# A Mamba block on one core: three tiles normalized inside the next tile's product, the first chunk's taps in one slot, later projections spread 1, 2, 1

## The chip, the cores and the metric

The kernel runs on one core of a Trainium2 chip. Times are device microseconds of one execution; the kernel before took 3516.83 us (median of three, 3515.82 to 3521.38). The engines are PE (TensorE, matrix products), PEld (its weight loads), DVE (VectorE), ACT (ScalarE), POOL (GpSimd) and SP, which only issues DMAs here. Each engine works through its instructions in a fixed order.

## The reference, cut to what matters

Four graph layers run one after the other on 3327 nodes with 256 features, each with a residual sum and a layer norm. The change lies in layer 1, a graph convolution followed by a Mamba block:

```python
h = jax.nn.relu(adj @ x @ gcn_w + gcn_b)
h = (h - mu) * lax.rsqrt(var + EPS) * ln_g + ln_b      # per node
xz = h @ w_in
xc, z = (xz[:, :D_INNER], xz[:, D_INNER:])             # D_INNER = 512
xconv = sum((xpad[k:k + L] * conv_w[:, k] for k in range(D_CONV))) + conv_b   # D_CONV = 4
u = jax.nn.silu(xconv)
dbc = u @ w_xp
dt = jax.nn.softplus(dbc[:, :DT_RANK] @ w_dt + b_dt)
# for each of 16 states, along the nodes: hst = exp(dt * A) * hst + dt * B * u;  y += hst * C
y = (ys + u * D_skip) * jax.nn.silu(z)
return y @ w_out
```

The nodes are a sequence for the Mamba block, so the scan over them cannot be cut without a carry.

## The kernel before, in words

**Tiles and chunks.** The 3327 nodes are 26 tiles of 128. `convolve` (L318) makes the graph convolution one tile at a time: 26 products of 128x128 by 128x256 over the adjacency (52 passes on PE), a copy to SBUF on ACT, two transposes, the product with `gcn_w`, the bias, relu with its sum, and the sum of squares. Three steps end a tile: `measure` (three small POOL instructions for the scale and the offset of the norm), `norm` (one ACT instruction) and `turn` (two PE transposes into the PSUM bank "ps", two ACT evacuations into the chunk's `hT`). `convolve` is a generator: it gives control back after each three products and reports units of work, 122 to a tile.

The scan takes the tiles in seven chunks of 3, 4, 4, 4, 4, 4 and 3 tiles. A chunk has 16 slots, one for each state. A slot does four scans on DVE (one per group of 128 channels, `scan`), each fed by a decay that ACT writes (`decay`, exp of dt times A, into one of two PSUM buffers), then one DVE product over all groups (`product`, buffer hc, two of them), which PE then adds up with transposing products into the y banks (`add_up`). POOL makes dt times u times B for the slot after the next (`feed`).

**The head of the next chunk.** While a chunk is scanned, `Head` prepares the next: `project` (four groups; PE product, ACT copy into `xc`, ACT first tap into `u`), `taps` (three DVE instructions for each group), `silu`, `mixed` (the product with `w_xp`, and two DMAs that write B and C out), `step_size`, `exponentials`, `rounding`, `logarithms`, `finish`. Chunk 0's own head runs before the scan begins. In which slot each step stands is the table `plan(c)` (L246): for chunk 0, one projection in each of slots 1 to 4, taps in slots 7, 8 and 9, silu 9, mixed 10; for later chunks, projections 0 and 1 in slot 5, 2 and 3 in slot 6, taps in slots 7 and 8. Before the projections of chunk c's slots the tiles of chunk c+1 must be there (`pump`). `gate_input` makes the z half of a tile. Projections, gate inputs, `mixed` and step sizes of the chunks from 2 on all go through the one bank "ps"; head 1 uses "y3" and "ps" in turn (`bank`, L298).

**What sets the order.** Before the scan loop the framework's list scheduler orders what is written. In the loop (`pinned`) DVE and POOL instructions keep the written order, and on ACT the decays, norms, silus and exponentials form one chain in written order (`in_turn`, L279). PE and the rest of ACT are ordered by the scheduler, mostly as written. How much of the convolution stream is written in each slot is the planner's: `duty` (L403) estimates the PE units of a slot (12 for a plain slot of chunk 0, 32 more with `mixed` there), `quota` (L422) fills the slots between two due times up to a common level, 96 units ahead. In the stream, the three end steps of a tile stand behind the next tile's third, seventh and eighth group of three products (the list `rest`, L374), but only in the loop. For tiles 0 to 6, which are written before it, they follow the tile at once (L375).

Of the kernel before, what the change touches and what calls it, by code (L numbers as in the profile page):

```python
# [18 lines left out]
P = 128  # L19
# [4 lines left out]
JC = 9  # L24
# [6 lines left out]
NG = DI // P  # L31
# [16 lines left out]
def gnn_kernel(ctx: ExitStack, tc: tile.TileContext, n: int, a: dict, out: bass.AP):  # L48
    nc = tc.nc
    nt = -(-n // P)  # L50
# [59 lines left out]
    def aggregate(atp, psum, it, rhs, cols, jh=JH, source=None):  # L110

        acc = psum.tile([P, cols], F32, name="acc")
        for j0 in range(0, nt, jh):
            m = min(jh, nt - j0)
            if source is not None:
                nc.sync.dma_start(rhs[:, j0:j0 + m, :D], source[:, j0:j0 + m, :])
            at = atp.tile([P, jh, P], F32, name="at")
            nc.sync.dma_start(at[:, :m, :], a["adjT"][it][:, j0:j0 + m, :])
            for j in range(m):
                nc.tensor.matmul(acc, at[:, j, :], rhs[:, j0 + j, :],  # L120
                                 start=(j0 + j == 0), stop=(j0 + j == nt - 1))
        return acc
# [35 lines left out]
    with tc.tile_pool(name="l1b", bufs=1) as wpool, tc.tile_pool(name="l1at", bufs=2) as l1at:  # L158
        X0 = F[:, :, :D]


        with tc.tile_pool(name="l0", bufs=1) as pool, tc.tile_pool(name="l0w", bufs=2) as work, \
# [4 lines left out]
            for it in range(nt):  # L167
                if it:
                    acc = aggregate(atp, psum, it, xa, D + 1)
                else:  # L170
                    acc = aggregate(atp, psum, it, xa, D + 1, J0, a["x"])
# [10 lines left out]
                for k in range(4):  # L182
                    nc.tensor.matmul(po, xt[:, k, :] if k < 2 else mt[:, k - 2, :], w0[:, k, :],
                                     start=(k == 0), stop=(k == 3))
# [7 lines left out]
        with tc.tile_pool(name="l1aw", bufs=1) as cwork, tc.tile_pool(name="l1c", bufs=2) as ch, \  # L192
# [53 lines left out]
            def plan(c):  # L246


                if c == 0:
                    return dict(project={g + 1: (g,) for g in range(NG)}, taps={7: (0,), 8: (1,), 9: (2, 3)}, gates={5: (0, 1), 6: (2,)},  # L250
                                silu=9, mixed=10, sizes={10: (0, 1), 11: (2, 3)}, exps=(11, 12), log=13)
                return dict(project={5: (0, 1), 6: (2, 3)}, taps={7: (0, 1), 8: (2, 3)}, gates={7: (0, 1), 8: (2, 3)},
                            silu=8, mixed=9, sizes={9: (0,), 10: (1, 2), 11: (3,)}, exps=(11, 12), log=13)

            ends = []
# [6 lines left out]
            pinned = False  # L262
# [13 lines left out]
            ten, act = nc.tensor, nc.scalar  # L276
# [29 lines left out]
            def spread(y, sm, nm, sq):  # L306

                act.activation(nm, sm, AF.Copy, scale=-1.0 / D)
                junk = cwork.tile([P, D], F32, name="m")
                act.activation(junk, y, AF.Square, bias=nm, accum_out=sq)  # L310

            def scales(rs, nb, nm, sq):

                gps.tensor_scalar(rs, sq, 1.0 / D, EPS, op0=ALU.mult, op1=ALU.add)
                gps.tensor_tensor(rs, rs, mhalf[:, :rs.shape[1]], op=ALU.pow)
                gps.tensor_tensor(nb, nm, rs, op=ALU.mult)

            def convolve():  # L318

                rest = []  # L320
                full = 0
                for it in range(nt):
                    if it < ends[1] // P and it % 2 == 0 and it:
                        cb = ypsum.tile([P, DI], F32, name="y3")
                    else:
                        cb = cpsum.tile([P, DI], F32, name="cb")
                    acc, tp = cb[:, :D], cb[:, D:]
                    for j in range(nt):
                        if j % JC == 0:
                            m = min(JC, nt - j)  # L330
                            at = l1at.tile([P, JC, P], F32, name="at")
                            nc.sync.dma_start(at[:, :m, :], a["adjT"][it][:, j:j + m, :])
                        ten.matmul(acc, at[:, j % JC, :], X0[:, j, :], start=(j == 0), stop=(j == nt - 1))  # L333
                        if j % JM == JM - 1 and j < nt - 1:
                            if rest:
                                step = rest.pop(0)
                                step()
                                full += step is turn
                            yield full, 4 * JM
                    m = cwork.tile([P, D], F32, name="m")  # L340
                    act.copy(m, acc)
                    yield full, 8
                    for k in range(2):
                        ten.transpose(tp[:, k * P:(k + 1) * P], m[:, k * P:(k + 1) * P], ident)
                    mt = cwork.tile([P, D], F32, name="m")
                    act.copy(mt, tp)
                    yield full, 4
                    for k in range(2):
                        ten.matmul(acc, mt[:, k * P:(k + 1) * P], gw[:, k, :], start=(k == 0), stop=False)
                    ten.matmul(acc, one, gb, start=False, stop=True)  # L350
                    h = cwork.tile([P, D], F32, name="hn")
                    rs, nb, nm, sm, sq = (small.tile([P, 1], F32, name=x) for x in ("rs", "nb", "nm", "sm", "sq"))
                    act.activation(h, acc, AF.Relu, accum_out=sm)  # L353
                    spread(h, sm, nm, sq)

                    def measure(rs=rs, nb=nb, nm=nm, sq=sq):
                        scales(rs, nb, nm, sq)

                    def norm(h=h, rs=rs, nb=nb):
                        turn_or_not = in_turn if pinned else lambda op, *x, **k: op(*x, **k)  # L360
                        turn_or_not(act.activation, h, h, AF.Identity, scale=rs, bias=nb)

                    def turn(it=it, h=h):
                        c = next(x for x in range(nch) if it * P < ends[x])
                        i = it * P - starts[c]
                        if i == 0:
                            hTs[c] = ch.tile([P, D // P, WC], F32, name="hT", bufs=3)
                        pt = psum.tile([P, WC], F32, name="ps")
                        for k in range(2):
                            ten.transpose(pt[:, k * P:(k + 1) * P], h[:, k * P:(k + 1) * P], ident)  # L370
                        for k in range(2):
                            act.activation(hTs[c][:, k, i:i + P], pt[:, k * P:(k + 1) * P], AF.Identity,
                                                 scale=g1[:, k:k + 1], bias=b1[:, k:k + 1])
                    rest = [*2 * [lambda: None], measure, *3 * [lambda: None], norm, turn]  # L374
                    if not pinned:  # L375
                        for step in (measure, norm, turn):
                            step()
                        rest = []
                        full += 1
                    yield full, 14  # L380
                for step in rest:
                    step()
                    full += step is turn
                    yield full, 12

            stream = convolve()
            done = taken = 0
            ready, valued, valuing = 0, 0, iter(())
# [14 lines left out]
            def duty(c, s):  # L403


                m, n, b = tiles_of(c), tiles_of(c + 1), tiles_of(c - 1)
                p = plan(c)
                return 4 * m * (2 if s == 0 else 1) + 24 * (1 <= s <= b) + 16 * len(gates(c, s)) \
                    + 4 * n * len(p["project"].get(s, ())) + 8 * n * (s == p["mixed"]) + 2 * n * len(p["sizes"].get(s, ()))
# [4 lines left out]
            def gates(c, s):  # L414
                return [i for i in plan(c)["gates"].get(s, ()) if i < tiles_of(c)]

            def due(c):
                return c * DS + min(plan(c)["project"]) if c else 8
# [263 lines left out]
            pinned = True  # L682
# [104 lines left out]
            pinned = False  # L787
# [6 lines left out]
            for i in range(m):  # L794
                it = starts[nch - 1] // P + i
# [819 lines left out]
```

## Time and profile before

| | |
|---|---|
| median of three | 3516.83 us |
| profiled execution | 3519.38 us, its span 3517.5 us |
| layer 0 (span's start to 380) | PE 371.6 of 380 us |
| first tiles of layer 1 (380 to 441.9) | PE 55.6, ACT 31.8 of 61.9 us |
| Mamba scan and its tail, to 1340 | DVE 821.0, PE 754.1, ACT 612.7, POOL 532.2 of 898.1 us |
| the rest (layers 2 and 3) | PE 2054.3, DVE 1470.3 of 2177.5 us |
| granted TensorE clock | 0.970 over the span |

The scan of chunk 0 begins at 441.9 us, chunk 1 at 588.4, chunk 2 at 728.5, chunk 3 at 868.6, chunk 4 at 1008.7, chunk 5 at 1146.5 and chunk 6 at 1277.7.

In the lines shown below, a line of the order of time gives the start and length in us, the engine, the source line, the operation, "out<-in", the shape and how many were merged; in brackets stands how long the engine stood idle before it and what ended that. Most DVE and POOL instructions of the loop, and the in-turn ones of ACT, carry a helper's line, L274 or L281, so that tile names tell them apart: h is a scan's output, hc the product's, u the taps', dA the decay. A line of who waited for whom gives the total us, the number of times and the longest.

### The profile page before, as it was taken

The numbers are of one execution on the slowest core, as the hardware profiler recorded it, in microseconds if no ns is written. First come the engines' busy times: TensorE is split into PE (matmuls) and PEld (weight loads), VectorE is DVE, ScalarE is ACT, GpSimd is POOL, SyncE is SP. The second block draws the span as 40 slices with busy tenths as digits, with TensorE's granted clock in tenths as the row PEclk, the third lists the DMA queues.
The fourth block names the chain that finished last, engine by engine and source line by source line (L and its number), as shares of the span: only waits on it lengthen the run. The fifth ranks groups of instructions, "written<-read, shape, count | busy, mean of one in ns | idle before, by whom it ended". The sixth has DMA issues, their size and how long they took to land. (4 is left out here: it accounts for less than half of the span.)

```text
span 3517.5 us, 43266 instructions
## 1 busy us (share of the span) xinstructions
PE 3235.5 (92%) x15597; PEld 2540.3 (72%) x15597; DVE 2370.4 (67%) x5245; ACT 1740.6 (49%) x2751; POOL 932.8 (27%) x942
## 2 busy tenths in 40 slices
PE   9999988988888766999899999999997999999996
PEld 7888766676676555888677878787775777777775
DVE  1111177999999997777454544444434999999996
ACT  0000356767667675111133333333336888888883
POOL 0000054666665653121100000000001243333332
PEclk9999998999999888999899999999999999999998
DMA  7443334334443222344321212121212112222220
GB/s 248 139 140 110 102 109 112 101 119 106 106 119 91 66 58 92 126 140 145 95 66 56 65 49 65 48 67 47 67 47 74 55 56 67 68 70 61 70 65 16
DMA packets 147577, 307.99 MB, mean 88 GB/s; under 512 B 19570, under 2 KB 68850, under 8 KB 147218
## 3 DMA queue, kind: packets, MB, share of 16 engines
q1 hardware_dynamic: 147346, 305.06, 29.7%
q8 instruction: 126, 2.06, 0.2%
q14 instruction: 105, 0.86, 0.1%
HBM read 294.36 MB, written 10.65 MB: 87 GB/s over the span
## 5 line engine op out<-in xcount | busy, mean ns | idle before, releaser
L274 POOL TENSOR_TENSOR h<-du,row 128x2048 f32<-128x2048 f32 (+1 forms) x110 | 465.7, 4233 | 339.3 <-DVE hc L274 270.8
L274 DVE TENSOR_TENSOR_SCAN h<-dA,carry,h 128x512 f32<-128x512 f32 (+1 forms) x384 | 448.7, 1220 | 19.8 <-ACT dA L281 19.7
L281 ACT ACTIVATE dA<-t,A_log 128x512 f32<-128x512 f32 (+1 forms) x448 | 292.3, 658 | 146.4 <-DVE h L274 143.4
L1058 PE MATMUL acc<-F,at 128*128 128x256 f32 x1352 | 353.5, 387 | 1.0 <-ACT q L832 0.6
L1091 PE MATMUL acc<-X,wt 128*128 128x256 f32 x1352 | 343.5, 390 | 10.5 <-ACT wt L1089 10.2
L1091 PE MATMUL acc<-G,wt 128*128 128x256 f32 x1352 | 336.8, 392 | 6.4 <-ACT wt L1022 5.9
L1091 PEld LDWEIGHTS acc<-X,wt 128*128 128x128 f32 x1352 | 242.6, 189 | 105.3 <-issue 41.3
L120 PE MATMUL acc<-xa,at 128*128 128x257 f32 x1352 | 308.6, 382 | 5.6 <-DMA at<-in_adjT 5.6
L1058 PE MATMUL acc<-X,at 128*128 128x256 f32 x1352 | 308.4, 381 | 0.0
L967 PE MATMUL acc<-F,at 128*128 128x257 f32 x1352 | 303.6, 381 | 1.2 <-DMA U<-in_U 1.2
L333 PE MATMUL cb<-F,at 128*128 128x256 f32 x1196 | 294.0, 394 | 7.4 <-ACT hn L353 4.5
L1091 PEld LDWEIGHTS acc<-G,wt 128*128 128x128 f32 x1352 | 250.1, 193 | 67.0 <-ACT wt L1022 36.8
L1103 DVE MAX8 cand<-e 128x8 f32<-128x128 f32 x676 | 142.2, 278 | 229.0 <-ACT e L1044 217.4
L1058 PEld LDWEIGHTS acc<-F,at 128*128 128x128 f32 x1352 | 237.9, 190 | 75.3 <-issue 50.2
L120 PEld LDWEIGHTS acc<-xa,at 128*128 128x128 f32 x1352 | 255.7, 191 | 42.4 <-issue 5.5
L1058 PEld LDWEIGHTS acc<-X,at 128*128 128x128 f32 x1352 | 252.9, 191 | 40.2 <-issue 7.0
L967 PEld LDWEIGHTS acc<-F,at 128*128 128x128 f32 x1352 | 253.4, 190 | 36.8 <-issue 1.4
L333 PEld LDWEIGHTS cb<-F,at 128*128 128x128 f32 x1196 | 228.8, 197 | 59.4 <-issue 14.3
L624 PE MATMUL y<-ident,hc 128*128 128x128 f32 x1664 | 229.7, 291 | 42.9 <-DVE hc L274 42.3
L624 PEld LDWEIGHTS y<-ident,hc 128*128 128x128 f32 x1664 | 204.5, 151 | 82.5 <-DVE hc L274 59.3
L274 DVE TENSOR_TENSOR hc<-h,row 128x2048 f32<-128x2048 f32 (+2 forms) x114 | 242.8, 2131 | 11.0 <-PE y L624 4.3
L1089 ACT COPY wt<-tp 128x512 f32<-128x512 f32 (+1 forms) x182 | 93.5, 557 | 309.2 <-PE tp L1087 309.0
(352 smaller groups left out, 5264.1 us busy)
## 6 DMA issues: line engine op xcount, KB each, us to landing
at<-in_adjT SPq DMA_DIRECT2D x102, 832.0 KB, 4.6
at<-in_adjT SPq DMA_DIRECT2D x260, 320.0 KB, 2.9
row<-bc SPq DMA_DIRECT2D x80, 512.0 KB, 5.1
at<-in_adjT SPq DMA_DIRECT2D x52, 576.0 KB, 4.0
at<-in_adjT SPq DMA_DIRECT2D x26, 512.0 KB, 3.8
row<-bc SPq DMA_DIRECT2D x32, 384.0 KB, 5.0
xt<-in_xT SPq DMA_DIRECT2D x26, 128.0 KB, 4.1
qd<-q SPq DMA_DIRECT2D x104, 32.0 KB, 1.9
```

Source lines behind the costliest of these rows:

```text
L120: nc.tensor.matmul(acc, at[:, j, :], rhs[:, j0 + j, :], start=(j0 + j == 0), stop=(j0 + j == nt - 1))
L274: return lambda *x, **k: tc.keep_in_program_order(op(*x, **k))
L281: decays.append(op(*x, **k))
L333: ten.matmul(acc, at[:, j % JC, :], X0[:, j, :], start=(j == 0), stop=(j == nt - 1))
L624: x = ten.matmul(y[:, g * P:(g + 1) * P], h[:, g, i * P:(i + 1) * P], ident, is_transpose=True, start=(first and g == 0), stop=(last and g ...
L967: nc.tensor.matmul(acc, at[:, j, :], F[:, j0 + j, :], start=(j0 + j == 0), stop=(j0 + j == nt - 1))
L1058: nc.tensor.matmul(acc, at[:, j, :], rhs[:, j0 + j, :], start=(j0 + j == 0), stop=(j0 + j == nt - 1))
L1089: copy(wt[:, :m, :], pt[:, :m, :])
L1091: nc.tensor.matmul(acc, wt[:, j, :], rhs[:, j0 + j, :], start=(j0 + j == 0), stop=(j0 + j == nt - 1))
L1103: nc.vector.max(cand[:, s * 8:(s + 1) * 8], z[:, s * SEG:(s + 1) * SEG])
```

## The change

There are three edits.

1. The end steps of tiles 3, 4 and 5 (those of chunk 1 but its last, tile 6) are no longer written at once: they go into the list and stand within the next tile's products. For these tiles, what a step puts on PE (the two transposes of `turn`) is kept behind the third product of its group.
2. In chunk 0 the taps of all four groups stand in slot 8 (before: one group in 7, one in 8, two in 9), silu in slot 8 and `mixed` in slot 9 (before: 9 and 10). The planner's duties of slots 9 and 10 change with it.
3. In the later chunks the projections stand in slots 5, 6 and 7 as 1, 2 and 1 groups (before: two and two in slots 5 and 6). Slot 7 holds the fourth behind its two gate inputs. Taps stay where they are.

```diff
                 if c == 0:
-                    return dict(project={g + 1: (g,) for g in range(NG)}, taps={7: (0,), 8: (1,), 9: (2, 3)}, gates={5: (0, 1), 6: (2,)},
-                                silu=9, mixed=10, sizes={10: (0, 1), 11: (2, 3)}, exps=(11, 12), log=13)
-                return dict(project={5: (0, 1), 6: (2, 3)}, taps={7: (0, 1), 8: (2, 3)}, gates={7: (0, 1), 8: (2, 3)},
+                    return dict(project={g + 1: (g,) for g in range(NG)}, taps={8: (0, 1, 2, 3)}, gates={5: (0, 1), 6: (2,)},
+                                silu=8, mixed=9, sizes={10: (0, 1), 11: (2, 3)}, exps=(11, 12), log=13)
+                return dict(project={5: (0,), 6: (1, 2), 7: (3,)}, taps={7: (0, 1), 8: (2, 3)}, gates={7: (0, 1), 8: (2, 3)},
                             silu=8, mixed=9, sizes={9: (0,), 10: (1, 2), 11: (3,)}, exps=(11, 12), log=13)
...
-                        ten.matmul(acc, at[:, j % JC, :], X0[:, j, :], start=(j == 0), stop=(j == nt - 1))
+                        mm = ten.matmul(acc, at[:, j % JC, :], X0[:, j, :], start=(j == 0), stop=(j == nt - 1))
                         if j % JM == JM - 1 and j < nt - 1:
                             if rest:
                                 step = rest.pop(0)
-                                step()
+                                with tc.issue_after(mm.ins) if it < ends[1] // P else nullcontext():
+                                    step()
                                 full += step is turn
...
                     rest = [*2 * [lambda: None], measure, *3 * [lambda: None], norm, turn]
-                    if not pinned:
+                    if not pinned and not (ends[0] <= it * P < ends[1] - P):
                         for step in (measure, norm, turn):
                             step()
                         rest = []
```

## The prediction

> **What bounds the kernel now.** I read first the table of engines by stage, then who waits for whom in the Mamba stage, then the order of time at the places where the waits are longest. The stretches below are the seven chunks of the Mamba scan (the columns are engine busy us and instruction counts, then the granted TensorE clock).
>
> ```profile
> core 0: us, PE busy (x) PEld busy (x) DVE busy (x) ACT busy (x) POOL busy (x), PEclk, DMA share, GB/s
> 441.90:588.40 146.50, 122.45 (x548) 90.13 (x547) 103.63 (x97) 87.86 (x174) 67.29 (x36) 0.90 0.40 104
> ...
> 728.50:868.60 140.10, 123.64 (x626) 93.37 (x625) 132.75 (x101) 97.61 (x190) 87.53 (x34) 0.96 0.40 110
> 868.60:1008.70 140.10, 123.63 (x627) 93.27 (x626) 132.73 (x101) 97.69 (x190) 87.56 (x34) 0.96 0.43 110
> ```
>
> From chunk 1 on DVE is the bound (132.7 of 140.1 us), with PE close behind. Chunk 0 is different: DVE works 103.6 of 146.5 us, and its waits are few and long:
>
> ```profile
> DVE h L274 <- ACT dA L281: 24.7, 7, 14.6
> DVE u L274 <- ACT u L492: 16.9, 1, 16.9
> ```
>
> ```profile
> 486.09 3.49 DVE L274 TENSOR_TENSOR_SCAN h<-dA,h 128x384 f32<-128x384 f32 x4
> ...
> 506.43 2.33 DVE L274 SCALAR_TENSOR_TENSOR u<-t,conv_w,u 128x512 f32<-128x512 f32 x3 [16.85 <-ACT u L492]
> ...
> 543.71 1.80 DVE L274 TENSOR_TENSOR_SCAN h<-dA,h 128x384 f32<-128x384 f32 x2 [14.64 <-ACT dA L281]
> ```
>
> The first is slot 7: the taps of group 0 stand in DVE's program order, and wait for head 1's projections, which need tiles 3 to 6. The second is slot 10: the decays stand behind the norm of tile 7 in ACT's chain. PE makes those tiles, and waits itself:
>
> ```profile
> PE ps L370 <- ACT hn L360: 11.9, 4, 4.5
> ```
>
> ```profile
> 452.00:457.00 5.00, 0.68 (x3) 0.68 (x4) 3.08 (x4) 1.28 (x4) 3.62 (x4) 0.70 0.35 97
> 457.00:461.00 4.00, 4.00 (x14) 3.14 (x13) 3.44 (x4) 2.95 (x6) 3.50 (x2) 0.52 0.24 66
> ...
> 477.00:481.00 4.00, 0.75 (x5) 0.34 (x4) 2.87 (x3) 1.17 (x4) 3.75 (x5) 1.00 0.63 170
> 481.00:485.00 4.00, 4.00 (x19) 3.66 (x18) 3.34 (x4) 3.16 (x8) 2.43 (x1) 0.57 0.27 91
> ```
>
> PE idles at the transposes of tiles 3, 4 and 5 (3.70, 4.54 and 3.25 us), and then runs 3 to 4 us at half clock.
>
> **Step 1: tiles 3 to 5 deferred.** Per tile three POOL instructions, one ACT norm, two PE transposes and two ACT evacuations move into the next tile's product; nothing is added and no DMA moves. PE loses 3.70+4.54+3.25 = 11.5 us of waiting, and the half clock after it: 6 us at 0.76, 4 at 0.52 and 4 at 0.57 cost 1.4+1.9+1.7 = 5.0. That is up to 16.5 us on PE's way to head 1. I take 12: tile 6 is not deferred, its POOL steps (0.45 us wait now, with POOL idle) can fall behind a 3.4 us feed, and PE's sums need DVE's products. At the worst a sum stays ahead of tile 6's last 20 passes and 4.4 us remain. Cover for the moved steps: on ACT the norm has some 5 us of product between measure and turn; on POOL the three instructions take 0.93 us and may stand behind one feed. SP's tile loads run over two buffers and stand behind row loads that wait for DVE; PE waited 1.4 us for them from 418 to 502, the price if that cover goes.
>
> The Trainium skill, page "TensorE: Matmul & The Clock Gate", section "Part 1: The HAM clock gate", puts the fall to half clock after an idle window of about 3.4 us. By it the 3.25 us wait would not slow PE, and the gain would be 1.7 us less; the row 481 to 485 shows 0.57 after it, so the row decides.
>
> **Step 2: all taps in slot 8, silu 8, mixed 9.** DVE does product 7 and scan 8 (1.75+3.49) before the taps. Norms in ACT's way cost slots 2 and 6 waits of 1.88+0.56+1.22+0.39 = 4.0 us, which I take as gone: DVE reaches the taps at 489.6-4+5.2 = 490.8. Group 0 of u was ready 5.5 us after the projection began at 500.88, so now at 500.9-12+5.5 = 494.4: a wait of 3.6 instead of 16.85. Taps 9.3, product 8, scan 9: product 9 starts at 509 instead of 525.6, a gain of 17. With 4.4 on PE it is 9; with 16.5, and DVE arriving at 490.8, 20. The twelve taps keep their 0.75 us each; for 9.3 us no scan runs, and PE fills that with tile 7's 52 passes (11.4 us). Silu and its two table loads (1.28 us each) move a slot, in the same number. Mixed issues its two small DMAs a slot earlier; SP's wait for them (5.2 us) moves along, ahead of row loads that have two slots of lead.
>
> The second wait: mixed adds 32 units to slot 9 and takes them from 10, so the planner's shares for slots 9 and 10 become 18 and 34 (were 50 and 2). Slot 9 then takes 24 units of stream instead of 60, slot 10 36 instead of 0, and tile 7's norm is written in slot 10, ahead of slot 11's decays and no longer slot 10's. PE from 489: projections 6.7, gates 6, tile 7 11.4, sums 3, mixed 3.4, tail and hand-overs 4: 523.5; relu, spread, POOL behind a feed, norm: 528. DVE could be there at 518; the wait left is 10. Before, it passed this point at 549: gain 21. Bounds: 9 (all of the wait stays) and 34 (all goes).
>
> Late next is PE: DVE may be two products ahead, and waited 4.3 us for that in chunk 1. PE begins tile 8 16 us earlier (540.6 to 524.5), and gains some 2.6 of half clock (8 us at 0.68) and 3 of waits for products: 21. So I give back 0, at most 5.
>
> **Step 3: projections 1, 2, 1.** Same instructions, later. In chunk 2:
>
> ```profile
> 789.69 1.88 PE L489 MATMUL ps<-hT,w_in 128*128 128x512 f32 x4
> 790.22 2.33 DVE L274 SCALAR_TENSOR_TENSOR u<-t,conv_w,u 128x512 f32<-128x512 f32 x3 [2.06 <-ACT u L492]
> ...
> 800.91 1.98 PE L568 MATMUL ps<-w_in,hT 128*128 128x512 f32 x4 [0.27 <-ACT sz L570]
> ```
>
> PE lags DVE by some 1.5 slots here: projections of slots 5 and 6 run in DVE's slot 7, and the taps of group 1 already wait 2.06 us. Group 1 now goes behind the whole sum of slot 6 and perhaps a product group: 1.1 to 2.6 us later. Group 3 trades places with the gate inputs in the one bank "ps" and goes where the second gate input ran, 801 to 803; copy 0.58 and u 0.82 bring it to 804.9, where DVE wanted it at 799.4+2.3 = 801.7. So 3.2 us per chunk. Chunks 1 to 4 have this lag (group 3 wanted at 663.1, 801.7, 941.7, 1080.3, ready some 3.2 later by the same working); chunk 5 lags less and pays nothing. 4 x 3.25 = 13. Bounds: 0 (the order leaves group 3 its old 5.6 us of margin) and 6.5 each (each of the six turns of the bank takes 4.5 us, as gate input 0 to 1 did in chunk 4). Queued behind the waiting taps on DVE are product and scans; PE and ACT wait for those. It adds up from chunk to chunk, since PE waits for ACT behind DVE's scans in each (4.61 us at 997).
>
> The Trainium skill, page "Perfetto Trace Analysis", section "Optimization Strategy", takes a gap that repeats as a sign of too few buffers. The 2.06 us gap repeats at 930, and the bank stays single, so by that rule spreading buys nothing and costs nothing, and the sum would be 21 us faster, 3496; the margins of the rows say otherwise.
>
> **Sum.** -21 + 13 = -8 us. The profiled execution took 3519.4 us (span 3517.5 and 1.9 around it), 2.6 above the median of three, so 3511.4 there and 3516.8-8 = 3509 at the median. What ends the Mamba stage moves the rest of the kernel alike.
>
> **The rivals.**
> - Spread hidden: group 3 keeps its margin. For it: chunk 1 had no tap wait at all. Against: one bank, one order. 3516.8-21 = 3496.
> - Slower, the bank's turns: each waits for ACT behind decays, 6.5 us per chunk, and the idle PE drops to half clock (4 us at 0.52, 1.8 more): 4 x 8.3 = 33, against 21: 3529. It decides from 7 us per chunk. For it: the copy of gate input 0 came 2.2 us after its product. Against: chunk 5's margin shows that a shorter lag ends it.
> - Step 1 does little: the sums pace PE, 9 of 21 remain, spread 13: 3521.
>
> **How the numbers follow.** A measurement tells about 0.2% (7 us) from no change. Forecast 0.40, own range 3503 to 3516 (0.22 of it faster by over 0.2%, 0.17 within, 0.01 slower); spread hidden 0.25, faster; bank's turns 0.22, slower; step 1 lost 0.13 (0.06 within, 0.07 slower). Faster 0.47, same 0.23, slower 0.30. The range goes from 3491 (hidden, with some of the 34) to 3530.
>
> **What would show it.** Right: no waits of PE for tiles 3 to 5's norms, clock near 1.0 from 430 to 490, the first projection at 489, a tap wait of 3 to 5 us in chunk 0, a decay wait of some 10 us in slot 11, tap waits of 1 to 3 us in slots 7 and 8 of chunks 1 to 4. Wrong: a projection still after 496; chunks 2 and 3 still 140.1 us apart (rival one) or above 147 (rival two).

## The result, and the profile after

The kernel after took 3544.99 us (median of four, 3543.90 to 3547.42), the kernel before, beside it, 3519.11 (median of four). The ratio is 1.0070, with a 95% interval of 1.0057 to 1.0083: slower by some 25 us, where 8 us faster was forecast, and outside the range of 3491 to 3530. The profiled execution has a span of 3542.6 us, 25.1 more than before.

The engines by stage, for chunks 0 to 3 of the kernel after (busy us and instruction counts, then the granted TensorE clock):

```profile
core 0: us, PE busy (x) PEld busy (x) DVE busy (x) ACT busy (x) POOL busy (x), PEclk, DMA share, GB/s
441.90:590.40 148.50, 127.92 (x554) 92.09 (x553) 104.08 (x97) 88.73 (x177) 68.33 (x37) 0.89 0.39 104
590.40:737.10 146.70, 128.23 (x617) 97.48 (x618) 132.16 (x101) 97.44 (x188) 86.71 (x34) 0.93 0.38 105
737.10:881.80 144.70, 123.46 (x627) 93.03 (x625) 132.76 (x101) 97.88 (x190) 86.96 (x35) 0.96 0.37 106
881.80:1030.30 148.50, 131.06 (x620) 99.53 (x621) 132.92 (x101) 97.70 (x190) 82.56 (x34) 0.90 0.40 104
```

DVE's work has not changed (132.76 us in chunk 2, before 132.75); the chunks got longer around it. From the end of each chunk's last product, the lengths in us:

| chunk | 0 (from 441.9) | 1 | 2 | 3 | 4 | 5 |
|---|---|---|---|---|---|---|
| before | 146.6 | 140.1 | 140.1 | 140.1 | 137.8 | 131.1 |
| after | 148.5 | 146.7 | 144.7 | 148.5 | 143.5 | 131.8 |

Chunk 0 gained nothing (+1.9), chunks 1 to 4 lost 6.6, 4.6, 8.4 and 5.7, chunk 5 lost 0.7: 27.9 us by the end of chunk 5, of which the rest of the span gave 2.8 back. These are lengths of one execution each: kernels with the same code for chunk 0 as before ended it between 588.5 and 592.9 us, so chunk 0's +1.9 lies within what single executions differ by.

**Chunk 0.** Who PE waited for between 418 and 506 us, after (us in total, times, longest):

```profile
PE y L625 <- DVE hc L274: 9.8, 6, 3.4
PE y L333 <- DMA at<-in_adjT: 3.2, 2, 2.8
...
PE ps L371 <- ACT hn L361: 0.4, 1, 0.4
```

The waits for the norms are gone as predicted (11.9 to 0.4). PE waits instead for DVE's products, in the sums (L625), 9.8 us where it was 0.4, and 3.2 for adjacency tiles. The order of time on PE shows the place (L333 is a tile's product, L625 a sum, L490 head 1's projections):

```profile
480.21 2.76 PE L333 MATMUL y<-F,at 128*128 128x256 f32 x12
486.35 2.82 PE L625 MATMUL y<-ident,hc 128*128 128x128 f32 x12 [3.38 <-DVE hc L274]
488.96 4.47 PE L333 MATMUL y<-F,at 128*128 128x256 f32 x12
493.27 1.47 PE L625 MATMUL y<-ident,hc 128*128 128x128 f32 x12
...
503.64 1.02 PE L490 MATMUL y<-hT,w_in 128*128 128x512 f32 x2
```

A sum stands behind most groups of twelve passes of a tile here, as it did before. PE needs some 4.1 us for such a group and a sum (2.76 and 1.47, of which the ends overlap), DVE 5.3 for a slot of four scans and a product (3.49 and 1.76), so PE is now early, and stops at the sum until DVE's product is there. The first projection starts at 503.64, before at 500.88. DVE, accordingly, first after, then one line of before:

```profile
509.20 9.04 DVE L274 SCALAR_TENSOR_TENSOR u<-t,conv_w,u 128x512 f32<-128x512 f32 x12 [14.24 <-ACT u L493]
523.67 1.80 DVE L274 TENSOR_TENSOR_SCAN h<-dA,h 128x384 f32<-128x384 f32 x2 [2.04 <-ACT dA L281]
537.98 0.96 DVE L274 TENSOR_TENSOR_SCAN h<-dA,h 128x384 f32<-128x384 f32 x1 [8.10 <-ACT dA L281]
545.64 1.80 DVE L274 TENSOR_TENSOR_SCAN h<-dA,h 128x384 f32<-128x384 f32 x2 [3.13 <-ACT dA L281]
573.37 1.80 DVE L274 TENSOR_TENSOR_SCAN h<-dA,h 128x384 f32<-128x384 f32 x2 [9.11 <-ACT dA L281]
```

```profile
571.40 1.80 DVE L274 TENSOR_TENSOR_SCAN h<-dA,h 128x384 f32<-128x384 f32 x2 [3.77 <-ACT dA L281]
```

The tap wait is 14.24 us, where the prediction had 3.6, and the decay waits behind it, which were 14.64 in slot 10 and 3.77 in slot 14, are four pieces with 22.4 us together (slots 9, 10, 11 and 14). The last of them grew most, from 3.77 to 9.11: DVE comes to slot 14 3.4 us sooner and is let go 2.0 us later.

**The later chunks.** DVE in chunk 2, after, then the taps of slot 8 before (both groups at once, with no wait; the wait in slot 7 was 2.06 us):

```profile
801.00 2.33 DVE L274 SCALAR_TENSOR_TENSOR u<-t,conv_w,u 128x512 f32<-128x512 f32 x3 [4.41 <-ACT u L493]
815.18 2.33 DVE L274 SCALAR_TENSOR_TENSOR u<-t,conv_w,u 128x512 f32<-128x512 f32 x3 [2.71 <-ACT u L493]
```

```profile
799.38 4.54 DVE L274 SCALAR_TENSOR_TENSOR u<-t,conv_w,u 128x512 f32<-128x512 f32 x6
```

The turns of the bank "ps" on PE at that place, after (L490 projections, L569 gate inputs, L625 sums into the y banks), and three of the projections before (L489; group 0, the second half of group 1, group 3):

```profile
790.59 1.88 PE L490 MATMUL ps<-hT,w_in 128*128 128x512 f32 x4
792.52 0.93 PE L625 MATMUL y<-ident,hc 128*128 128x128 f32 x7
...
795.26 1.20 PE L625 MATMUL y<-ident,hc 128*128 128x128 f32 x9
...
797.62 1.88 PE L490 MATMUL ps<-hT,w_in 128*128 128x512 f32 x4
800.63 1.88 PE L490 MATMUL ps<-hT,w_in 128*128 128x512 f32 x4
...
804.10 1.88 PE L569 MATMUL ps<-w_in,hT 128*128 128x512 f32 x4
808.02 1.98 PE L569 MATMUL ps<-w_in,hT 128*128 128x512 f32 x4 [0.74 <-ACT sz L571]
...
811.70 1.98 PE L490 MATMUL ps<-hT,w_in 128*128 128x512 f32 x4 [0.82 <-ACT sz L571]
```

```profile
782.16 1.88 PE L489 MATMUL ps<-hT,w_in 128*128 128x512 f32 x4
...
787.42 1.12 PE L489 MATMUL ps<-hT,w_in 128*128 128x512 f32 x2
...
792.71 1.88 PE L489 MATMUL ps<-hT,w_in 128*128 128x512 f32 x4
```

Group 1's projection starts 7.0 us after group 0's, with a whole sum between, and ends 8.9 us after that start. Before, it started 2.7 us after group 0's, but was cut in two by the end of a tile and ended after 6.4. The taps of slot 7 wait 4.41 us for it instead of 2.06. Group 3's runs 11.1 us after group 2's (before, 3.0: 792.71 against 789.69), behind both gate inputs, each of which keeps the bank for some 3.8 us; the taps of slot 8 wait another 2.71, where there was no wait. Over chunks 1 to 4 the tap waits come to 25.1 us, before 4.7: that is 20.4 of the 25.3 us that these chunks lost. The rest lies in smaller waits.

### The profile page after: what moved, and what is told of

Read it like the earlier page. It is cut to its first block, busy times and chain, and to the rows that moved or that the text cites. A ratio compares the mean times of both kernels' runs of the same rounds, so it can differ in the third digit from the quotient of the medians.

```text
span 3542.6 us, 43259 instructions
## 1 busy us (share of the span) xinstructions
PE 3259.6 (92%) x15597; PEld 2560.2 (72%) x15597; DVE 2371.4 (67%) x5245; ACT 1743.3 (49%) x2751; POOL 919.5 (26%) x942
## 3 DMA queue, kind: packets, MB, share of 16 engines
q8 instruction: 126, 2.06, 0.2%
## 5 line engine op out<-in xcount | busy, mean ns | idle before, releaser
L274 DVE TENSOR_TENSOR_SCAN h<-dA,carry,h 128x512 f32<-128x512 f32 (+1 forms) x384 | 449.0, 1221 | 25.1 <-ACT dA L281 25.1
L1092 PEld LDWEIGHTS acc<-X,wt 128*128 128x128 f32 x1352 | 242.6, 189 | 105.2 <-issue 41.3
L333 PE MATMUL cb<-F,at 128*128 128x256 f32 x1196 | 296.1, 394 | 4.0 <-ACT hn L354 3.4
L625 PE MATMUL y<-ident,hc 128*128 128x128 f32 x1664 | 241.3, 301 | 57.7 <-DVE hc L274 57.6
L625 PEld LDWEIGHTS y<-ident,hc 128*128 128x128 f32 x1664 | 212.2, 155 | 101.8 <-DVE hc L274 79.0
L333 PEld LDWEIGHTS cb<-F,at 128*128 128x128 f32 x1196 | 230.5, 199 | 58.5 <-issue 19.1
```

Source lines behind the costliest of these rows:

```text
L274: return lambda *x, **k: tc.keep_in_program_order(op(*x, **k))
L333: mm = ten.matmul(acc, at[:, j % JC, :], X0[:, j, :], start=(j == 0), stop=(j == nt - 1))
L625: x = ten.matmul(y[:, g * P:(g + 1) * P], h[:, g, i * P:(i + 1) * P], ident, is_transpose=True, start=(first and g == 0), stop=(last and g ...
L1092: nc.tensor.matmul(acc, wt[:, j, :], rhs[:, j0 + j, :], start=(j0 + j == 0), stop=(j0 + j == nt - 1))
```

## The experiments

Theory A: in chunk 0 PE is held by the sums that the scheduler puts between a tile's products, so that edits 1 and 2 buy nearly nothing; the spread makes the whole loss. The rival theory: edits 1 and 2 gain some 20 us as predicted, and the spread costs that much more. All times below are medians, ratios are against the kernel before on the same chip (medians of 3521.1 to 3521.4 us), with 95% intervals.

### Each edit alone, and two together

Edit 1 alone (the deferred tiles, with the old tables; the diff's second and third hunk):

```diff
-                    if not pinned:
+                    if not pinned and not (ends[0] <= it * P < ends[1] - P):
```

> Only the first edit: tiles 3 to 5 deferred, both slot tables as before. Theory A (the sums of chunk 0's products, which the scheduler puts between the product groups, pace PE, so that the removed norm waits come back as waits for DVE's products): PE's waits for the norms go from 11.9 to under 1 us, its waits for hc from 0.4 to about 10 us, the first projection of head 1 stays between 497 and 505 us, time within 5 us of before. Theory B (the deferral gains, and gathering the taps in slot 8 gives it away): first projection by 492 us, time 8 to 15 us below before.

Measured: 3517.87 us, ratio 0.9983 (0.9973 to 0.9994). PE between 418 and 506 us:

```profile
PE y L625 <- DVE hc L274: 9.5, 5, 3.4
PE y L333 <- DMA at<-in_adjT: 3.5, 2, 3.1
...
PE ps L371 <- ACT hn L361: 0.5, 1, 0.5
```

The exchange of norm waits for product waits is edit 1's own, as theory A had it. One sum shows it best, first before, then with edit 1:

```profile
473.78 1.53 PE L624 MATMUL y<-ident,hc 128*128 128x128 f32 x12 [0.38 <-DVE hc L274]
```

```profile
473.73 1.47 PE L625 MATMUL y<-ident,hc 128*128 128x128 f32 x12
```

Here PE was spared the wait for tile 4's norm (4.54 us) and came no sooner. Before, the products of slots 0 to 6 were ready 0.05, 5.26, 1.56, 0.21, 0.05, 2.48 and 0.84 us ahead of their sums; the two large margins stand behind the norm waits. With edit 1 all seven are 0.05 to 0.5: PE takes each sum as soon as DVE has made it. The first projection came at 501.26, no sooner than before (500.88), and the tap wait was 17.20. The small gain comes later: the decay waits fell from 24.7 to 19.4 us, and chunk 0 ended at 584.1 (before 588.5).

Edit 2 alone:

```diff
-                    return dict(project={g + 1: (g,) for g in range(NG)}, taps={7: (0,), 8: (1,), 9: (2, 3)}, gates={5: (0, 1), 6: (2,)},
-                                silu=9, mixed=10, sizes={10: (0, 1), 11: (2, 3)}, exps=(11, 12), log=13)
+                    return dict(project={g + 1: (g,) for g in range(NG)}, taps={8: (0, 1, 2, 3)}, gates={5: (0, 1), 6: (2,)},
+                                silu=8, mixed=9, sizes={10: (0, 1), 11: (2, 3)}, exps=(11, 12), log=13)
```

> Only the second edit: chunk 0's taps all in slot 8, silu 8, mixed 9. Theory A: the wait at the taps shrinks by about a slot (5 us), the decay wait of slot 10 splits into several that sum to about the same; time 0 to 8 us below before. Theory B: 10 to 18 us above before.

Measured: 3520.78 us, ratio 1.0001 (0.9991 to 1.0011). The tap wait fell from 16.85 to 13.87, and the decay waits rose from 24.7 to 27.4: 41.3 us of waiting against 41.6, moved and not removed. Chunk 0 ended at 590.0. That is theory A, with 3 us off the tap wait instead of 5 and nothing off the time.

Edit 3 alone:

```diff
-                return dict(project={5: (0, 1), 6: (2, 3)}, taps={7: (0, 1), 8: (2, 3)}, gates={7: (0, 1), 8: (2, 3)},
+                return dict(project={5: (0,), 6: (1, 2), 7: (3,)}, taps={7: (0, 1), 8: (2, 3)}, gates={7: (0, 1), 8: (2, 3)},
```

> Only the third edit: projections of the later chunks 1, 2, 1. Theory A (this edit makes the whole loss): chunks 1 to 4 each 4.5 to 8.5 us longer, with tap waits of 2 to 4.5 us in slot 7 and about 2.7 us in slot 8, time 22 to 28 us above before. Theory B (the prediction's price of 3.25 us per chunk holds, the rest of the loss is chunk 0's): 11 to 15 us above before.

Measured: 3542.87 us, ratio 1.0062 (1.0044 to 1.0079). The chunks 1 to 5 took 147.1, 147.6, 146.4, 142.3 and 132.1 us, and the two tap waits of chunk 2 were 4.41 and 2.72 us, as in the kernel after. The spread makes the loss: 21.5 us by the medians, just under the 22 to 28 of theory A, where theory B had 11 to 15.

Edits 1 and 2 together:

> The first two edits together, without the spread projections. Theory A: chunk 0 ends within 4 us of before, chunks 1 to 4 are 140 us again, time within 5 us of before. Theory B: 8 to 14 us above before. The prediction's own price of the first two edits was 21 us below before.

Measured: 3518.40 us, ratio 0.9991 (0.9982 to 1.0001). PE waited 10.3 us for products, the first projection came at 504.12, the tap wait was 13.70. Where the prediction had 21 us from the two, 0 to 6 came. The rival theory is out.

### What PE is paced by in chunk 0

Edit 1 with the old tables, and the sums of chunk 0's slots 1 to 7 without their priority over the tile's products:

```diff
                 if added:
-                    with tc.high_priority() if s == 0 or c == 0 else nullcontext():
+                    with tc.high_priority() if s == 0 or (c == 0 and s > 7) else nullcontext():
                         summed = add_up(*added)
```

> Kernel before with the first edit, and the sums of chunk 0's products in slots 1 to 7 at the common priority, so that the scheduler puts the products of tiles 4 to 6 ahead of them on PE. Theory A (the sums paced PE): PE waits less than 2 us for hc up to the first projection, which comes by 488 us; DVE waits instead in slot 2 or 3, where both product buffers are full, for about 20 us, and has no long wait after it; chunk 0 ends 5 to 12 us sooner than before, time 4 to 12 us below before. Theory B (something else holds PE): first projection still after 497 us, time 10 us or more above before, as DVE has lost its early slots.

Measured: 3510.53 us, ratio 0.9973 (0.9963 to 0.9982): faster than both kernels. In this run PE's waits from 418 to 506 us, and DVE's first long stop:

```profile
PE y L333 <- DMA at<-in_adjT: 3.8, 2, 3.5
PE ps L371 <- ACT hn L361: 3.7, 2, 2.0
...
PE y L625 <- DVE hc L274: 0.4, 1, 0.4
```

```profile
477.62 1.76 DVE L274 TENSOR_TENSOR hc<-h,row 128x1536 f32<-128x1536 f32 x1 [17.51 <-PE y L625]
...
533.22 1.80 DVE L274 TENSOR_TENSOR_SCAN h<-dA,h 128x384 f32<-128x384 f32 x2 [4.18 <-ACT dA L281]
```

PE no longer waits for products, the first projection is at 482.00, and chunk 0 ends at 579.4, 9.1 us sooner than before. But DVE's 17 us stop stays and only changes its reason: with two product buffers, DVE stands until PE takes up the sums again. So the 19 us that PE won are not DVE's; what DVE won is the shorter decay waits (15.4 against 24.7 us). Theory A held.

The same edit of the sums without any deferred tile:

> The kernel before, with one edit: the sums of chunk 0's slots 1 to 7 at common priority; no tile is deferred. The run with deferral and late sums took 3510.5 (0.9973 of before) and had its first projection at 482.0. If deferral and the place of the sums are each needed (PE is held by whichever of the two is left), PE still waits some 10 to 12 us for the norms of tiles 3 to 6, the first projection of head 1 comes at 494 to 501, and the time is 3517 to 3522. If the place of the sums alone made that gain, the first projection comes before 487 and the time is 3508 to 3513, and deferring is worth nothing in any order.

Measured: 3514.05 us, ratio 0.9984 (0.9975 to 0.9994). PE still waits for the norms, and its projections come early all the same:

```profile
PE ps L370 <- ACT hn L360: 9.7, 4, 4.3
```

```profile
485.68 1.13 PE L489 MATMUL y<-hT,w_in 128*128 128x512 f32 x2
```

This corrects theory A in one point, and neither alternative of the expectation held. Most of the advance of the projections (15.2 of 18.9 us) needs no deferred tile. Between 441.9 us and the first projection PE's groups show where it is from: sums 4.4 us instead of 12.0, passes of tiles 26.3 instead of 31.6 (108 instead of 124, the others now behind the projection), norm waits 6.0 instead of 8.2. Deferring the tiles adds 3.7 us to that, and nothing while the sums keep their places. Whether it still adds to the time is not separated: 0.9973 and 0.9984 have overlapping intervals; chunk 0 ended at 583.1 here and at 579.4 with the tiles deferred.

Edit 2 on top of both (tiles deferred, sums late, taps in slot 8):

> The kernel before with edits 1 and 2 (tiles 3 to 5 deferred, taps in slot 8), and the sums of chunk 0's slots 1 to 7 at common priority. If the prediction's second step holds once PE is no longer paced by the sums, the decay waits of slots 10 to 14 (4.18, 2.69 and 2.19 us without edit 2) shrink, and chunk 0 ends 3 to 8 us before 579.4: 3503 to 3508. If edit 2 only moves work between slots whose wait is for PE anyway, DVE's one long wait stays at 15 to 18 us, chunk 0 ends at 578 to 584, and the time is 3509 to 3515.

Measured: 3515.64 us, ratio 0.9990 (0.9980 to 0.9999). DVE's stop for the sums stayed at 17.52 us, chunk 0 ended at 584.2, about as the second alternative had it (578 to 584, and 3509 to 3515). The decays:

```profile
526.17 1.80 DVE L274 TENSOR_TENSOR_SCAN h<-dA,h 128x384 f32<-128x384 f32 x2 [1.76 <-ACT dA L281]
...
538.75 0.96 DVE L274 TENSOR_TENSOR_SCAN h<-dA,h 128x384 f32<-128x384 f32 x1 [5.93 <-ACT dA L281]
...
567.09 1.80 DVE L274 TENSOR_TENSOR_SCAN h<-dA,h 128x384 f32<-128x384 f32 x2 [3.78 <-ACT dA L281]
```

The waits in chunk 0 (from 441.9 to 592 us, each run's own; the first column is the tap wait, or the stop for the sums in the last three) add up so:

| | first stop | decays | sum | chunk 0 ends |
|---|---|---|---|---|
| before | 16.9 | 24.7 | 41.6 | 588.5 |
| edit 1 | 17.2 | 19.4 | 36.6 | 584.1 |
| edit 2 | 13.9 | 27.4 | 41.3 | 590.0 |
| edits 1 and 2 | 13.7 | 24.9 | 38.6 | 589.3 |
| after | 14.2 | 27.9 | 42.1 | 590.4 |
| sums late | 20.4 | 17.5 | 37.9 | 583.1 |
| edit 1, sums late | 17.5 | 15.4 | 32.9 | 579.4 |
| edits 1 and 2, sums late | 17.5 | 17.0 | 34.5 | 584.2 |

Each row is one execution. The four kernels that leave the code of chunk 0 alone (edit 3 alone, and the three runs of the next section without edits 1 and 2) had 24.3 to 26.4 us of decay waits there and ended it at 589.5 to 592.9, so some 2 us of waits and 4 us of the end are no difference. Edit 2 shortens the first stop by 3.5 us at most and adds 2.7, 5.5 and 1.6 to the decays in the three pairs that differ by it alone; only the 5.5 is clear of that. That edit 2 gains nothing is shown. That it costs something is not: in each pair the intervals of the ratios overlap.

Why a shorter first stop does not end the chunk sooner is seen on ACT. These are the norms of tile 8, after and before:

```profile
572.27 0.60 ACT L281 ACTIVATE hn<-hn,nb,rs 128x256 f32<-128x256 f32 x1 [1.21 <-POOL nb L274]
```

```profile
570.30 0.60 ACT L281 ACTIVATE hn<-hn,nb,rs 128x256 f32<-128x256 f32 x1 [1.21 <-POOL nb L274]
```

The decay that slot 14 waits for stands behind this norm in ACT's chain. In all eight runs of the table the last long wait of chunk 0 ends 1.1 us after this norm starts, and the chunk 17.7 to 18.2 us after it. In the kernel after the norm waits for a tile that PE finishes late (ACT stood idle 2.81 us for it just before), so what DVE saves ahead of slot 14 it loses there, and edits 1 and 2 did not bring PE to tile 8 sooner. A part of edit 2's decay waits has another place: in the kernel after, ACT works off eight instructions of the step sizes from 528.7 to 536, partly waiting for PE, ahead of the decay of slot 10 that DVE gets at 537.98. What of the table (all taps at once, `mixed` a slot earlier, the shares of the planner) is at fault was not tried apart.

### Which group of the spread costs

Group 3 alone one slot later:

```diff
-                return dict(project={5: (0, 1), 6: (2, 3)}, taps={7: (0, 1), 8: (2, 3)}, gates={7: (0, 1), 8: (2, 3)},
+                return dict(project={5: (0, 1), 6: (2,), 7: (3,)}, taps={7: (0, 1), 8: (2, 3)}, gates={7: (0, 1), 8: (2, 3)},
```

> Kernel before with only the fourth projection moved: 2 in slot 5, 1 in slot 6, 1 in slot 7 behind the gate inputs. Theory A (each later projection has its own wait: slot 7's taps wait for group 1, slot 8's for group 3 behind two turns of the one bank): slot 7 keeps its wait of about 2 us, slot 8 gets one of 3 to 5 us, 10 to 16 us above before. Theory B (only group 1's place counts, group 3 has margin): within 4 us of before.

Measured: 3547.87 us, ratio 1.0083 (1.0066 to 1.0100), some 27 us above before, as much as the whole spread or more. Neither theory had this size; A had the waits, but at 3 to 5 us. Chunks 1 to 5 took 145.8, 146.6, 146.3, 142.5 and 136.5 us: 23.1 us lost in the first four, and 5.4 in chunk 5, which stays unexplained. The taps of slot 7 are as before, those of slot 8 wait 5.4 to 6.8 us:

```profile
797.61 2.33 DVE L274 SCALAR_TENSOR_TENSOR u<-t,conv_w,u 128x512 f32<-128x512 f32 x3 [2.06 <-ACT u L492]
815.85 2.33 DVE L274 SCALAR_TENSOR_TENSOR u<-t,conv_w,u 128x512 f32<-128x512 f32 x3 [6.77 <-ACT u L492]
```

Group 1 alone later, with group 3 in its old slot:

```diff
-                return dict(project={5: (0, 1), 6: (2, 3)}, taps={7: (0, 1), 8: (2, 3)}, gates={7: (0, 1), 8: (2, 3)},
+                return dict(project={5: (0,), 6: (1, 2, 3)}, taps={7: (0, 1), 8: (2, 3)}, gates={7: (0, 1), 8: (2, 3)},
```

> Kernel before with only the second projection moved: 1 in slot 5, 3 in slot 6, none in slot 7. Theory A: slot 7's tap wait grows from 2 to about 4.4 us, slot 8 has none, 8 to 13 us above before. Theory B: 20 us or more above before, as the whole spread.

Measured: 3529.56 us, ratio 1.0035 (1.0023 to 1.0048). Chunks 1 to 5 took 143.4, 143.5, 142.7, 140.7 and 130.5 us: 3.3, 3.4, 2.6 and 2.9 lost in the first four. In chunk 2 the taps waited once, 4.42 us in slot 7. Theory A held.

The spread of the change, with the fourth projection written ahead of slot 7's gate inputs:

```diff
-                        uses += first
+                        uses = first + uses if s == 7 else uses + first
```

> The spread 1, 2, 1, but in slot 7 the fourth projection is written ahead of the two gate inputs, so it takes the bank two turns sooner. Theory A (bank turns): no wait of slot 8's taps, slot 7's stays 4 us, so that it equals the run with the second projection late, 8 to 13 us above before. Theory B (the planner's shifted stream units make the loss): as the spread itself, about 21 us above before.

Measured: 3530.09 us, ratio 1.0032 (1.0021 to 1.0043), chunks of 143.3, 143.1, 142.6, 142.0 and 132.9 us. One tap wait was left in chunk 2:

```profile
797.16 2.33 DVE L274 SCALAR_TENSOR_TENSOR u<-t,conv_w,u 128x512 f32<-128x512 f32 x3 [4.41 <-ACT u L492]
```

So the wait in slot 8 is made by the two turns that the gate inputs have in the bank, and goes when group 3 has its turn ahead of them; what remains equals group 1's price (3.3, 3.4, 2.6 and 2.9 us per chunk there, 3.2, 3.0, 2.5 and 4.2 here). The same units of the planner stand in this run as in the spread itself, so theory B is out. The two prices do not add up. In chunks 1 to 4 group 1 alone cost 12.2 us, group 3 alone 23.1, and both 25.3. A DVE that has waited 2.35 us longer in slot 7 comes that much later to slot 8, and its wait there is 2.71 us instead of 5.4 to 6.8. Late group 3 therefore makes nearly the whole loss by itself; with it in place, group 1 adds little, and without it group 1 costs some 3 us per chunk.

## Why the prediction was wrong, point by point

- **What bounds the kernel now** held from chunk 1 on: DVE. For chunk 0 it named two stops of DVE and took each for a gain; what ends the chunk is the norm of tile 8, which lets slot 14's decays go.
- **Step 1** failed, and with it the forecast. That the norm waits go was right (11.9 to 0.4 us). "I take 12" off PE's way was wrong, and even the bound "4.4 us remain" was too high: edit 1 alone moved the first projection by +0.4 us. The working summed PE's waits and took them off, without following PE to the instruction that then comes last. It did name it ("PE's sums need DVE's products") and then gave it the bound, not the value. At the sum of 473.78 us, behind two of the three removed waits, PE had 0.05 us of margin left: what it got ahead it lost in the sums, 9.5 us where it had been 0.4, and 3.5 at tile loads that had been priced 1.4. The half clock came back too: the stretch from 482 to 492 us of the kernel after has a granted clock of 0.68.
- **Step 2** failed on Step 1's account and on its own. The tap wait of 3.6 hung on projections at 489; they came at 503.64, and it measured 14.2. "The wait left is 10" measured 22.4 in four pieces: tile 7's norm, put at 528, ran at 544.54 (before 542.61). And where the projections did come at 482, the table of edit 2 gained nothing either: chunk 0 ended at 584.2 with it, at 579.4 without. "Gain 21" measured, for edits 1 and 2, 3 us of the total, with an interval of 6 down to nothing.
- **Step 3** had its mechanism right, taps that wait for turns of the one bank, and its term was mis-sized: 3.25 us per chunk against 6.6, 4.6, 8.4 and 5.7 measured, mean 6.3, near its upper bound of 6.5; chunk 5 paid 0.7, where nothing was forecast. Two things made it too small. Group 3 moved alone made waits of 5.4 to 6.8 us in slot 8, where 3.2 were forecast, and cost 5.8 us per chunk: it ran 13.6 to 15.3 us after group 2, not the 11.2 that the second gate input had before, since PE waited 1.8 to 2.0 us for the copy of the first gate input. And group 1's "1.1 to 2.6 us later" was worked out, measured 2.35 (4.41 against 2.06), and then left out of the sum; alone it costs 3.0 per chunk. In the whole change group 3 did run 11.1 us after group 2 and was waited for 2.7 us, close to the 3.2. That is luck: group 2 and DVE were both late there, behind the wait for group 1 that the sum did not have.
- **The rivals.** "The bank's turns" came nearest, in its price per chunk (8.3) and in its mechanism: the copies that waited behind ACT's other work show with group 3 alone. The lower clock shows in chunks 3 and 4 of the kernel after (0.90 and 0.92, before 0.96 and 0.99). Its point of decision, 7 us per chunk, counted on the 21 us of Steps 1 and 2. "The sums pace PE" was right as a mechanism, with 0 to 6 us left instead of 9. That PE's sums and a dearer spread come together is a case to which the prediction gave no chance.
- **The repeated gap.** The Trainium skill, page "Perfetto Trace Analysis", section "Optimization Strategy", says that the same gap repeating can mean too few buffers. The prediction made of it, and weighed against Step 3, that the spread costs nothing; the page does not say that, and edit 3 alone cost 0.62%. With the bank as single as before, the order of its turns alone made and removed the gap in slot 8. Whether a second bank would remove it too was not tried.

## What to carry to other kernels

Before a wait of an in-order engine is booked as a gain, follow that engine to its next instructions and ask of each when its operand was ready in the old trace: here the product of a sum two norm waits further on had been ready 0.05 us ahead of it, and the sums took back all that the norms gave. When a stop is shortened, look also for the next one that ends at a time of its own: here DVE's stop in slot 14 ended with a norm that nothing had brought forward. And each delay that the working finds must be carried on to the next consumer, not added to its price nor dropped: late group 1 cost 12.2 us alone, late group 3 23.1, both together 25.3. In a buffer with a single slot, write the user that is waited for ahead of those that are not: that alone took back half of the spread's loss.

## What the runs showed of the hardware

- The stops that replaced the norm waits halved PE's clock in places. In the kernel after, behind 3.38 us of waiting, twelve transposes took 2.82 us and twelve passes 4.47, where they took 1.47 and 2.76 a few microseconds away: 1.35 + 1.71 = 3.1 us lost. With edit 1 alone, and with edits 1 and 2, a stop of the same 3.38 us cost 1.8 and 1.6. The length of a stop does not decide alone: behind 3.10 us the granted clock was 0.62 with edit 1 alone (462 to 466.5 us) and 1.00 in the kernel after (463 to 466), and there 2.79 us of waiting for a tile load were followed by 0.50 (435 to 441). The Trainium skill, page "TensorE: Matmul & The Clock Gate", section "Part 1: The HAM clock gate", has the clock halve after at least one idle window of some 3.4 us; the stops named here are shorter than that, as was the one of 3.25 us in the kernel before, and most of them were followed by a lowered clock.
- Some DVE instructions took 1 us more than their like. In the run with edits 1 and 2 and late sums, first POOL, then DVE:

```profile
548.10 3.45 POOL L274 TENSOR_TENSOR h<-du,row 128x1536 f32<-128x1536 f32 x1 [2.96 <-DMA row<-bc]
554.34 3.44 POOL L274 TENSOR_TENSOR h<-du,row 128x1536 f32<-128x1536 f32 x1 [2.80 <-DMA row<-bc]
```

```profile
550.32 2.84 DVE L274 TENSOR_TENSOR hc<-h,row 128x1536 f32<-128x1536 f32 x1
...
556.49 3.44 DVE L274 SCALAR_TENSOR_TENSOR t<-t 128x2048 f32<-128x2048 f32 x1
```

The product that starts at 550.32, with POOL busy for another 1.23 us, takes 1.09 us longer than the usual 1.75; the instruction at 556.49, with 1.29 us of POOL ahead, takes 1.17 longer than the 2.27 that it took with edit 1 and late sums. The Trainium skill, page "SBUF — State Buffer", section "SBUF: two separate sides", says that a DVE operation with two SBUF inputs and a POOL operation that reads SBUF exclude each other for whole instructions. Both rows fit that: the second is `rounding`, which reads two buffers that the listing both calls t. The other runs agree. In the twelve kernels of this case, from 440 to 1280 us, 90 such instructions (the products, and SCALAR_TENSOR_TENSOR t<-t) began while one POOL feed was still at work, and each took longer than its like by what was left of the feed less 0.11 to 0.15 us. Ten more, the first products of chunk 0, began under the opening feed's pieces and were longer too, by 0.1 to 2.3 us. None of the 1179 others took over 0.03 us more than usual, 122 of them with a feed that began while they ran. So a feed of POOL that a late `row` shifts onto the start of DVE's product costs DVE the overlap.
